# Expert results stored by token through an indirect transfer, and read back as plain rows

## The chip, the cores and the metric

The kernel runs on one core of a Trainium2 chip. The core has five engines that run side by side and meet only through semaphores: the matrix engine (PE), the vector engine (DVE), the scalar engine (ACT), the GpSimd engine (POOL) and the sync engine (SP), whose work here is to issue transfers. Transfers are issued by SP, ACT or POOL and carried out by 16 DMA engines. A transfer whose rows are picked by a list of indices is always issued by POOL in this kernel (`indirect_dma_start`). The metric is the device time of one execution, in microseconds (us); lower is better.

## The reference

Four images of 384 channels and 32 x 32 positions pass through two layers, all in fp32. Layer 0 is attention with relative-position tables and a factored feed-forward block. Layer 1 is a depthwise 7x7 convolution and a mixture of experts over the tokens (one token for each position, 4096 in all). What matters for this change is the mixture:

```python
scores = jnp.einsum('bsd,de->bse', x, gate_w) + gate_b
probs = jax.nn.softmax(scores, axis=-1)
topk_vals, topk_idx = jax.lax.top_k(probs, TOP_K)        # 2 of 4 experts
...
masked = masked / (jnp.sum(masked, axis=-1, keepdims=True) + 1e-09)
h = jax.nn.gelu(jnp.einsum('bsd,edh->ebsh', x, w1) + b1[:, None, None, :], approximate=False)
y = jnp.einsum('ebsh,ehd->ebsd', h, w2) + b2[:, None, None, :]
out = jnp.einsum('bse,ebsd->bsd', masked, y)
```

The kernel computes only the two experts that each token chose. So a token has two result rows of 384 numbers, and its output is the sum of the two, each times its gate.

## The kernel before, in words

**The phases.** `qkv_phase` normalises the input and computes queries, keys and values, eight steps of 512 tokens. In its steps 2 to 5 it also writes zeros over `xs_d`, a DRAM tensor with room for every expert's list of tokens (4 x 4096 rows of 384 numbers, L186 to L190). `attention_phase` is the longest phase. `rest_phase` holds everything after it: projection and feed-forward (`front`), the convolution on DVE (`convolve`, L984) and the experts.

**From tokens to blocks.** For each image, `gates` chooses the experts, and `slot_positions` (L683) gives every token-expert pair a place in that expert's list. `scatter` (L1121) then writes the normalised token rows to these places in `xs_d`, 16 indirect transfers of 128 rows for each image (`write`, L1102). `block_list` (L758) cuts the lists into blocks of 128 rows of one expert. There are 67 blocks in four groups of 13, 16, 16 and 22; group b can start once the rows of image b have landed, for which the loads wait through `after` (L857, used in L1151).

**A block.** `blocks` (L1141) works through a group. `fetch` (L1145) gathers a block's 128 rows into `xg` by an indirect transfer. `turn` (L1155) transposes them on PE and copies them out on ACT as `xT`. Twelve rounds over the hidden units follow: three matmuls (`e_ps`, L1198), a gelu on ACT (`eh`, L1201), a matmul into `y_ps` (L1176). The weights come in halves of 2.5 MB, again by indirect transfers on POOL (`weights`, L1164); where a buffer already holds that expert's half, the indices lie outside and nothing is moved. After the last round, `second` adds the bias on DVE into `yo` (L1179), and SP stores `yo` to rows n to n+127 of `y_d`, so the results lie in the order of the blocks (L1181).

**Back to tokens.** `result_rows` (L736) works out on DVE, from the ranks kept for each image and the `pieces` that `block_list` kept, in which row of `y_d` each token's two results lie. `combine` (L1213) takes 256 tokens at a time: `results` gathers the two rows of each token with four indirect transfers on POOL (L1237) and loads the residual; `weigh` scales and adds (ACT L1249, DVE L1250); `finish` transposes on PE (L1226), adds the residual on DVE (L1227) and stores the output (L1228). Images 0 to 2 are combined in the last group, from its seventh block on (`NOT_LAST`), between the matmuls of the blocks; image 3 is combined after the last block, with all its 16 gathers issued at once.

**What sets the order.** `others` yields small pieces of the next image's work, and `more` (L1357) hands them out between the rounds of a block, by an account of estimated DVE and PE time. Within an engine, the framework's scheduler may move an instruction ahead of one that it expects to wait; across engines only semaphores order the work. Each engine carries out its own queue strictly in order, so an instruction that waits holds up all that is behind it. POOL's queue in `rest_phase` holds the scatters, the gathers of rows, the weight loads and the gathers of results; SP's holds the loads of `front`, the stores of `yo`, the residual loads and the output stores.

Of the kernel before, what the change touches and what calls it, by code (L numbers as in the profile page):

```python
# [47 lines left out]
CAP = B * N  # L48

# [16 lines left out]
def token_stats(nc, pools, ident, x, eps, rows=None, step=4):  # L66
# [5 lines left out]
    for j in range(nj):  # L72
# [6 lines left out]
        if rows is not None:  # L79
            nc.scalar.copy(rows[j], ps[:, :C])  # L80
# [40 lines left out]
def qkv_phase(tc, cst, x, w_qkv, qk_d, v_d, xs_d):  # L121
# [6 lines left out]
    with ExitStack() as es:  # L128
# [7 lines left out]
        zero = wp.tile([P, 1, C], F32, name="zero")  # L136
# [546 lines left out]
def slot_positions(nc, pools, cst, image, count, total):  # L683


    small, psum = pools
# [12 lines left out]
    rank, pos = image["rank"], new(shape, "pos")  # L699
# [15 lines left out]
    for i, pick in enumerate(chosen(nc, new, mask)):  # L715
        for src, dst in ((pos, fpos), (top, image["gate"])):
            nc.vector.tensor_tensor(prod, pick, src, ALU.mult)
            nc.vector.tensor_reduce(dst[:, :, i : i + 1], prod, AX.X, ALU.add)
    nc.vector.tensor_copy(image["pos"], fpos)
# [14 lines left out]


def result_rows(nc, small, image, pieces):  # L736


    shape = list(image["mask"].shape)

    def new(shape, name):
        return small.tile(shape, F32, tag=f"p_{name}", name=f"p_{name}", bufs=1)

    pos, part, step = new(shape, "pos"), new(shape, "prod"), new([P, 1, NEXP], "step")
    nc.vector.tensor_tensor(pos, image["rank"], bcast(pieces[0][1].unsqueeze(1), 1, shape[1]), ALU.add)
    for (_, off0), (lo, off) in zip(pieces, pieces[1:]):
        nc.vector.tensor_tensor(step[:, 0, :], off, off0, ALU.subtract)
        nc.vector.tensor_tensor(part, image["rank"], bcast(lo.unsqueeze(1), 1, shape[1]), ALU.is_ge)
        nc.vector.tensor_tensor(part, part, bcast(step, 1, shape[1]), ALU.mult)
        nc.vector.tensor_tensor(pos, pos, part, ALU.add)  # L750
    row = new([P, shape[1], 2], "fpos")
    for i, pick in enumerate(chosen(nc, new, image["mask"])):
        nc.vector.tensor_tensor(part, pick, pos, ALU.mult)
        nc.vector.tensor_reduce(row[:, :, i : i + 1], part, AX.X, ALU.add)
    nc.vector.tensor_copy(image["pos"], row)


def block_list(nc, small, cst, group, parts, done):  # L758
# [24 lines left out]
    for i, (lo, _, falling) in enumerate(parts):  # L783
        turn = slice(None, None, -1) if falling else slice(None)
        begin, off = group["pieces"][i]
        nc.vector.tensor_scalar(begin, lo, float(BLK), None, ALU.mult)
        nc.vector.tensor_scalar(
            off, first[:, i * NEXP : (i + 1) * NEXP, 0][:, turn], float(group["start"]), float(BLK), ALU.add, ALU.mult
        )
        nc.vector.tensor_tensor(off, off, begin, ALU.subtract)  # L790
# [20 lines left out]
    nc.vector.scalar_tensor_tensor(where, over, OUTSIDE, where, ALU.mult, ALU.add)  # L811
    nc.vector.tensor_scalar(where, where, slot[:, 0:1], cst["wrow"][:, 0:1], ALU.add, ALU.add)
# [22 lines left out]
def rest_phase(tc, cst, x, ao_d, ins, xs_d, y_d, x2_d, out):  # L835
# [9 lines left out]
    with ExitStack() as es:  # L845
# [31 lines left out]
        pc = {"before": const("before", [P, P]), "blocks": const("blocks", [P, MAXB]), "wrow": const("wrow", [P, 2])}  # L877
        pc["one"], pc["slot0"] = one, const("slot0", [P, NEXP])
# [181 lines left out]
        for b, nb in enumerate(COUNTS):  # L1060
# [3 lines left out]
                "rank": new([P, nj, NEXP], f"rank{b}"),  # L1064
# [6 lines left out]
                "pieces": [  # L1071
                    (new([P, NEXP], f"begin{b}{i}"), new([P, NEXP], f"off{b}{i}")) for i in range(1 + (b + 1 == B))
                ],
# [8 lines left out]
        scattered = []  # L1082

        def gates(b):
# [9 lines left out]
            for j, row in enumerate(rows):  # L1094
                nc.scalar.activation(row, row, AF.Identity, bias=shift[:, j, :], scale=rstd[:, j, :])
                im["rows"].append(row)
            yield 0.0, 0.0

        def new_row():
            return hid.tile([P, C], F32, tag="rows", name="rows", bufs=16)  # L1100
# [20 lines left out]
        def scatter(b, pause):  # L1121
            im, g = images[b], groups[b]
            slot_positions(nc, (small, ps_m), pc, im, counts[b], counts[b + 1])
            yield 4.0, 0.5
            for j, rows in enumerate(im["rows"]):
                for s in range(2):
                    write(rows, im["pos"][:, j, s : s + 1])
# [13 lines left out]
        def blocks(g, more):  # L1141
# [3 lines left out]
            def fetch(k):  # L1145
                xg = ld.tile([P, C], F32, tag="xg", name="xg")
# [8 lines left out]
            def turn(k):  # L1155
# [6 lines left out]
                xT[k] = t  # L1162
# [11 lines left out]
            def second(k, ff, hs, w, py):  # L1174
                o = WB + ff % FH * C
                nc.tensor.matmul(py, hs, w[:, o : o + C], start=(ff == 0), stop=(ff == NF - 1))  # L1176
                if ff == NF - 1:
                    yo = hid.tile([P, C], F32, tag="yo", name="yo", bufs=2)
                    nc.vector.tensor_tensor(yo, py, w[:, WB + FH * C :], ALU.add)  # L1179
                    n = (g["start"] + k) * BLK  # L1180
                    nc.sync.dma_start(y_d[n : n + BLK, :], yo)  # L1181
# [5 lines left out]
            for k in range(g["nb"]):  # L1187
                py = ps_y.tile([P, C], F32, tag="y", name="y_ps", bufs=2)
                for ff in range(NF):
# [6 lines left out]
                    for c in range(KC):  # L1196
                        o = c * FH * P + f * P
                        nc.tensor.matmul(ph, w[:, o : o + P], xT[k][:, c, :], start=(c == 0), stop=(c == KC - 1))  # L1198
# [14 lines left out]
        def combine(bs):  # L1213
# [4 lines left out]
            y_rows = y_d if end else y_d[: (groups[-1]["start"] + NOT_LAST) * BLK]  # L1218
            pieces = [p for g in groups for p in g["pieces"]]
# [10 lines left out]
            def results(b, n0):  # L1230

                zs = []
                for j in range(2):
                    ys = [new_row() for _ in range(2)]
                    for i, y in enumerate(ys):
                        index = images[b]["pos"][:, n0 // P + j, i : i + 1]
                        nc.gpsimd.indirect_dma_start(y, None, y_rows, bass.IndirectOffsetOnAxis(ap=index, axis=0))  # L1237
# [8 lines left out]
            def weigh(b, n0, zs):  # L1246
                for j, (z, y) in enumerate(zs):
                    gate = images[b]["gate"][:, n0 // P + j, :]
# [225 lines left out]
```

## Time and profile before

| | |
|---|---|
| median of 3 runs | 3289.18 us (3285.77 to 3293.74) |
| profiled execution | 3284.5 us, span 3282.7 us from first to last instruction |
| PE busy | 2986.8 us, 91% of the span, 25591 matmuls |
| DVE busy | 1991.4 us, 61% |
| ACT busy | 1331.7 us, 41% |
| POOL busy | 1159.6 us, 35% |
| mean granted clock of PE | 0.968 |
| store of `yo` to `y_d` | 67 transfers of 192 KB, issued by SP |
| gathers of results from `y_d` | 64 indirect transfers, issued by POOL |
| zeros to `xs_d` | 8 transfers of 3072 KB, issued by POOL |

The shares are averages over stages with quite different limits. The stages are, by the trace: the qkv phase up to about 237 us, attention up to about 1660 us, the first image's front and convolution up to about 1905 us, the blocks of the experts from there to 3251 us with the other images' fronts and convolutions between them up to about 2600 us, and the last image's combine up to 3282.7 us. Busy time in the views does not count the issue of plain transfers[...].

### The profile page before, as it was taken

The numbers are of one execution on the slowest core, as the hardware profiler recorded it, in microseconds if no ns is written. First come the engines' busy times: TensorE is split into PE (matmuls) and PEld (weight loads), VectorE is DVE, ScalarE is ACT, GpSimd is POOL, SyncE is SP. The second block draws the span as 40 slices with busy tenths as digits, with TensorE's granted clock in tenths as the row PEclk, the third lists the DMA queues.
The fourth block names the chain that finished last, engine by engine and source line by source line (L and its number), as shares of the span: only waits on it lengthen the run. The fifth ranks groups of instructions, "written<-read, shape, count | busy, mean of one in ns | idle before, by whom it ended". The sixth has DMA issues, their size and how long they took to land.

```text
span 3282.7 us, 64040 instructions
## 1 busy us (share of the span) xinstructions
PE 2986.8 (91%) x25591; PEld 2063.8 (63%) x25591; DVE 1991.4 (61%) x3619; ACT 1331.7 (41%) x2687; POOL 1159.6 (35%) x1100
## 2 busy tenths in 40 slices
PE   8998998989898989999879888998999999999996
PEld 4445666666675656666643445575577777777775
DVE  2227777768676877777748659998999730001101
ACT  1115656555555655565511131342443333233322
POOL 2225536263536364544520032123125231114422
PEclk9999999999999999999989998998999999999998
DMA  3786464545455555646240313261156035474852
GB/s 140 268 300 195 102 194 115 179 122 174 117 174 129 169 136 141 171 120 187 74 153 23 113 66 142 80 257 56 44 209 234 27 115 213 152 277 151 303 208 70
DMA packets 222202, 500.60 MB, mean 152 GB/s; under 512 B 92192, under 2 KB 145056, under 8 KB 214224
## 3 DMA queue, kind: packets, MB, share of 16 engines
q1 hardware_dynamic: 156720, 214.75, 21.4%
q0 software_dynamic: 43552, 228.24, 18.8%
q10 hardware_dynamic: 21632, 53.52, 6.4%
q8 instruction: 202, 3.31, 0.4%
q14 instruction: 96, 0.79, 0.1%
HBM read 543.58 MB, written 152.37 MB: 212 GB/s over the span
## 4 chain that ended last, share of the span: by engine, by line
PE 65%; DVE 12%; issue 8%; ACT 7%; DMA 5%; POOL 3%; SPq 1%; another core or an unknown queue 0%; ACTq 0%; POOLq 0%; DVEq 0%
PE e_ps L1198 14%; PE y_ps L1176 13%; DVE xb L993 7%; PE av_ps L215 6%; PE t_ps L406 6%; PE tabq_ps L215 5%; PE sc_ps L215 4%; PE tv_ps L215 3%; ACT arow L387 3%; PE tabk_ps L215 2%; PE qk_ps L163 2%; ACT aT L407 2%; PE a_ps L416 2%; DVE oT L470 2%; DMA qs<-qk_d 1%
## 5 line engine op out<-in xcount | busy, mean ns | idle before, releaser
L349 POOL TENSOR_TENSOR bias<-b,s 128x416 f32<-128x416 f32 (+24 forms) x656 | 660.0, 1043 | 631.8 <-DMA s<-sd 424.5
L1198 PEld LDWEIGHTS e_ps<-xT,w 128*128 128x128 f32 x4824 | 654.6, 192 | 230.5 <-issue 16.7
L1198 PE MATMUL e_ps<-xT,w 128*128 128x128 f32 x4824 | 672.6, 277 | 20.2 <-DVE xb L906 8.0
L1176 PE MATMUL y_ps<-w,eh 128*128 128x384 f32 x1608 | 652.5, 490 | 17.7 <-ACT eh L1201 14.3
L993 DVE SCALAR_TENSOR_TENSOR xb<-img,c_w,xb 128x1024 f32<-128x1024 f32 (+1 forms) x539 | 611.0, 1196 | 0.0
L1201 ACT ACTIVATE eh<-e_ps,w 128x128 f32<-128x128 f32 x804 | 293.3, 367 | 753.8 <-PE e_ps L1198 692.3
L1166 POOL DMA_INDIRECT w<-in_w,row x134 | 164.0, 1224 | 786.4 <-PE y_ps L1176 270.7
L377 DVE CUSTOM_DVE_ANT_0 arow<-sc_ps,bias 128x1024 f32<-128x1024 f32 x256 | 312.8, 1222 | 191.4 <-POOL bias L349 101.9
L398 DVE TENSOR_REDUCE extra<-arow 128x32 f32<-128x32 f32 (+24 forms) x768 | 378.7, 551 | 30.2 <-ACT arow L387 30.2
L406 PEld LDWEIGHTS t_ps<-ident,arow 128*128 128x128 f32 x2048 | 226.4, 144 | 265.0 <-ACT arow L387 185.3
L407 ACT COPY aT<-t_ps 128x512 f32<-128x512 f32 x512 | 275.5, 589 | 267.4 <-PE t_ps L406 241.9
L387 ACT ACTIVATE arow<-arow,nm 128x1024 f32<-128x1024 f32 x256 | 297.0, 1160 | 177.6 <-DVE nm L377 166.5
L406 PE MATMUL t_ps<-ident,arow 128*128 128x128 f32 x2048 | 289.1, 286 | 74.4 <-ACT arow L387 73.3
L215 PE MATMUL sc_ps<-kk,qs 48*32 48x512 f32 x4096 | 294.0, 625 | 50.8 <-DMA qs<-qk_d 26.8
L1179 DVE TENSOR_TENSOR yo<-y_ps,w 128x384 f32<-128x384 f32 x67 | 37.2, 556 | 446.9 <-PE y_ps L1176 439.7
L1176 PEld LDWEIGHTS y_ps<-w,eh 128*128 128x128 f32 x1608 | 248.0, 193 | 31.1 <-ACT eh L1201 16.9
L215 PEld LDWEIGHTS av_ps<-aT,vb 128*64 128x64 f32 x4096 | 222.3, 137 | 52.3 <-ACT aT L407 37.8
L303 DVE STREAM_TRANSPOSE b<-tabk_ps 128x480 f32<-128x480 f32 x256 | 219.1, 1000 | 44.5 <-PE tabk_ps L215 24.8
L215 PE MATMUL av_ps<-aT,vb 128*64 128x128 f32 x4096 | 237.7, 274 | 0.0
L215 PE MATMUL tabk_ps<-tab,kq 48*128 48x480 f32 x512 | 225.7, 588 | 3.3 <-DVE b L303 3.3
L215 PE MATMUL tabq_ps<-tab,kq 48*128 48x480 f32 x512 | 224.5, 585 | 0.7 <-ACT va L177 0.7
L308 ACT COPY st<-tabq_ps 128x480 f32<-128x480 f32 x256 | 141.8, 561 | 75.3 <-PE tabk_ps L215 36.5
(212 smaller groups left out, 3190.4 us busy)
## 6 DMA issues: line engine op xcount, KB each, us to landing
sd<-st SPq DMA_DIRECT2D x128, 480.0 KB
s<-sd SPq DMA_DIRECT2D x512, 120.0 KB
xs_d<-zero POOLq DMA_DIRECT2D x8, 3072.0 KB
tvw<-in_tv ACTq DMA_DIRECT2D x120, 192.0 KB
y_d<-yo SPq DMA_DIRECT2D x67, 192.0 KB
qk_d<-qk_sb POOLq DMA_DIRECT2D x48, 256.0 KB
qs<-qk_d SPq DMA_DIRECT2D x256, 48.0 KB
kq<-qk_d ACTq DMA_DIRECT2D x56, 192.0 KB
```

Source lines behind the costliest of these rows:

```text
L215: ins = nc.tensor.matmul(*args, **kw)
L303: turn = nc.vector.transpose(b2.rearrange("p e y x -> p x (e y)")[:, i + j], ps[:, j, : SPAN * IMG])
L349: nc.gpsimd.tensor_tensor(bias[:, y0:y1, :], bass.AP(b2.tensor, b2.offset + (e * IMG + y0) * IMG, [list(b2.ap[0]), [(step * IMG + 1) * IMG ...
L377: nc.vector.tensor_tensor_reduce(s["flat"], ps.rearrange("p h n -> p (h n)"), s["bias"].rearrange("p y x -> p (y x)"), -SCALE, BIG, ALU.ad ...
L387: nc.scalar.activation(s["flat"], s["flat"], AF.Exp, bias=s["nm"], scale=-1.0, accum_out=dn[:, y % YT : y % YT + 1])
L398: pin(nc.vector.tensor_reduce(ex[:, i, :], a[:, p0:p1, :].rearrange("p y x -> p x y"), AX.X, ALU.add))
L406: pin(nc.tensor.transpose(pt[:, j, :], s["flat"][:, k0 : k0 + P], ident))
L407: pin(nc.scalar.copy(aT[:, 4 * g : 4 * g + 4, s["y"] % YB, :], pt))
L993: nc.vector.scalar_tensor_tensor(acc[:, k, y0:y1], img[:, k, dy + y0 : dy + y1, dx : dx + IMG], w7[:, k, dy, dx : dx + 1], acc[:, k, y0:y1 ...
L1176: nc.tensor.matmul(py, hs, w[:, o : o + C], start=(ff == 0), stop=(ff == NF - 1))
L1198: nc.tensor.matmul(ph, w[:, o : o + P], xT[k][:, c, :], start=(c == 0), stop=(c == KC - 1))
L1201: nc.scalar.activation(hs, ph, AF.Gelu, bias=w[:, o : o + 1])
```

## The change

The result of a block no longer goes to the block's rows, but to its token's rows: `z_d` has two rows for each token, row 2t for the first of its two experts and 2t+1 for the second.

- **Rows carry their address.** The rows of `xs_d` become 386 numbers long (`CX`). `scatter` appends two numbers to each row: twice the token's index less `OUTSIDE`, and the list start of the token's first expert. The token numbers come as a constant. `slot_positions` computes the second with two more DVE operations, `scatter` the first with one, and ACT copies both into the row (one small copy for each 128 rows). The zeros written over `xs_d` have the new row length too.
- **A block works out where its rows go.** In `turn`, two small DVE operations on 128 x 1 numbers compare the block's expert with the row's first expert and add up the row of `z_d`; empty slots end up outside and are skipped.
- **The store.** `second` stores `yo` with an indirect transfer on POOL, in place of the plain one on SP.
- **The loads.** `results` loads every second row of 256 rows of `z_d` with plain transfers: on SP, and in the last image's combine half of them on ACT. They wait, through `after`, for the stores of the blocks that can hold their tokens (`written`).
- **Removed.** `result_rows`, the `pieces` and the `rank` that it needed, and `y_d`. The combine of images 0 to 2 starts once the stores of all the blocks that can hold their tokens are issued, which is at the same block as before.

```diff
-        zero = wp.tile([P, 1, C], F32, name="zero")
+        zero = wp.tile([P, 1, CX], F32, name="zero")
...
+        if i == 0:
+            nc.vector.tensor_tensor(prod, pick, bcast(cst["slot0"].unsqueeze(1), 1, nj), ALU.mult)
+            nc.vector.tensor_reduce(image["ids"][:, :, 1:2], prod, AX.X, ALU.add)
...
-def result_rows(nc, small, image, pieces):
...
+    nc.vector.tensor_scalar(group["over"], over, OUTSIDE, OUTSIDE, ALU.mult, ALU.add)
+    nc.vector.tensor_scalar(group["first"], expert, float(CAP), None, ALU.mult)
...
+            nc.vector.tensor_scalar_add(im["ids"][:, :, 0], pc["token"], 2.0 * b * N)
             yield 4.0, 0.5
             for j, rows in enumerate(im["rows"]):
+                nc.scalar.copy(rows[:, C:], im["ids"][:, j, :])
...
-                xT[k] = t
+                at = small.tile([P, 1], F32, tag="at", name="at")
+                nc.vector.tensor_tensor(at, g["first"][:, k, :], xg[:, C + 1 :], ALU.is_gt)
+                to = small.tile([P, 1], U32, tag="to", name="to", bufs=3)
+                nc.vector.scalar_tensor_tensor(to, at, g["over"][:, k, :], xg[:, C : C + 1], ALU.add, ALU.add)
+                xT[k] = t, to
...
-                    n = (g["start"] + k) * BLK
-                    nc.sync.dma_start(y_d[n : n + BLK, :], yo)
+                    stored.append(nc.gpsimd.indirect_dma_start(
+                        to_z.pop(), bass.IndirectOffsetOnAxis(ap=xT.pop(k)[1], axis=0), yo, None,
+                        bounds_check=2 * NT - 1, oob_is_err=False,
+                    ))
...
-                        index = images[b]["pos"][:, n0 // P + j, i : i + 1]
-                        nc.gpsimd.indirect_dma_start(y, None, y_rows, bass.IndirectOffsetOnAxis(ap=index, axis=0))
+                        r0 = 2 * (b * N + n0 + j * P) + i
+                        queue = nc.scalar if end and i else nc.sync
+                        load = queue.dma_start(y[:, :C], from_z[r0 : r0 + 2 * P - 1 : 2, :])
+                        for other in written:
+                            after(load, other)
...
-            if not end:
-                for b in (*bs, B - 1):
-                    result_rows(nc, small, images[b], pieces)
-                    yield 3.0, 0.0
...
-            if g is groups[-1] and k == NOT_LAST and "combined" not in g:
+            if len(stored) == groups[-1]["start"] + NOT_LAST and "combined" not in groups[-1]:
                 g["combined"] = combine(range(B - 1))
...
-    xs_d = dram.tile([NEXP * CAP, C], F32, name="xs_d")
-    y_d = dram.tile([ALL * BLK, C], F32, name="y_d")
+    xs_d = dram.tile([NEXP * CAP, CX], F32, name="xs_d")
+    z_d = dram.tile([2 * NT, C], F32, name="z_d")
```

## The prediction

> **What bounds the kernel now.** I read the page's shares first (PE busy 91% of 3282.7 us), then the busy time of each engine by stage, and then the timeline wherever a stage touches the change. By stage:
>
> ```profile
> 150.00:160.00 10.00, 7.56 (x19) 3.23 (x17) 0.00 (x0) 1.40 (x3) 1.61 (x3) 1.00 1.01 359
> ...
> 2160.00:2260.00 100.00, 93.45 (x541) 69.22 (x539) 98.86 (x201) 36.59 (x85) 31.06 (x26) 0.98 0.52 196
> 2660.00:2760.00 100.00, 100.00 (x616) 79.81 (x615) 3.63 (x8) 30.20 (x81) 22.05 (x22) 1.00 0.52 194
> 2960.00:3060.00 100.00, 97.27 (x607) 77.89 (x607) 15.12 (x27) 33.89 (x88) 43.78 (x44) 1.00 0.59 213
> 3252.00:3283.00 31.00, 7.57 (x24) 4.25 (x24) 8.76 (x16) 4.92 (x8) 15.46 (x16) 0.55 0.53 156
> ```
>
> The columns are the stretch, its length, then busy us of PE, PE's weight loads, DVE, ACT and POOL, PE's clock, the DMA engines' share and GB/s. From 2660 to 2960 PE is never idle: what the change adds to POOL or DVE there costs nothing, and what it takes from SP brings nothing. Four places are not covered by PE: the qkv phase after 120 us (DMA engines full, PE idle), the conv stretch to about 2260 (DVE full), the combine of images 0 to 2 (small PE gaps), and the end, where PE works 7.6 of 31 us.
>
> The end, from the timeline:
>
> ```profile
> 3250.38 0.56 DVE L1179 TENSOR_TENSOR yo<-y_ps,w 128x384 f32<-128x384 f32 x1 [13.89 <-PE y_ps L1176]
> 3253.64 0.97 POOL L1237 DMA_INDIRECT rows<-y_d,pos  x1 [31.68 <-issue]
> ...
> 3256.81 0.61 ACT L1249 ACTIVATE rows<-rows,gate 128x384 f32<-128x384 f32 x1 [7.94 <-DMA rows<-y_d,pos]
> ...
> 3272.72 0.96 POOL L1237 DMA_INDIRECT rows<-y_d,pos  x1 [0.30 <-issue]
> ```
>
> The store takes 2.70 us from the end of `yo` to the first gather; then POOL issues 16 gathers, one in 1.27 us, until 3273.7. ACT and DVE work a row as it lands. POOL's issue is the limit.
>
> The start of group 1:
>
> ```profile
> 2236.86 1.02 POOL L1103 DMA_INDIRECT xs_d<-rows,pos  x1 [21.77 <-DVE b_first L782]
> ...
> 2245.20 0.54 DVE L1179 TENSOR_TENSOR yo<-y_ps,w 128x384 f32<-128x384 f32 x1
> ...
> 2261.81 1.02 POOL L1147 DMA_INDIRECT xg<-xs_d,slot  x1 [1.01 <-DMA xs_d<-rows,pos]
> ...
> 2265.04 0.88 PE L1160 MATMUL xT_ps<-ident,xg 128*128 128x128 f32 x3 [7.52 <-DMA xg<-xs_d,slot]
> ```
>
> A chain from DVE over POOL to PE: PE stands 7.52 us. What is added ahead of it on DVE or POOL comes out of PE's time.
>
> [...] an indirect issue takes about 1.0 us with DVE idle and up to 2.1 us beside the convolution, while the convolution's operation keeps its 1.28 us.
>
> **The change part by part.** All against the profiled execution (span 3282.7, time 3284.5); the median of the runs, 3289.2, lies 4.7 above, and I carry the difference over to it.
>
> *The end, -8.5 us.* `yo` ends at 3250.94. The scatter waits on nothing else in POOL's queue: 0.1 for the semaphore, 1.0 to issue, and 2.36 to land (row above: the last scatter of image 1 was issued by 2259.45, the gather waiting for it started at 2261.81). Loads start at 3254.4, 0.8 later than the gathers. A plain issue takes 0.32 us (the store's row); eight on SP and eight on ACT are out after 3 to 5 us instead of 20. The first pair lands at about 3257, as before, but ACT issues its eight first and turns to scaling at about 3258.5. After that two limits: DVE has 8 x 0.62 + 4 x 1.02 = 9.0 us and about 2.5 us of waits for PE's transposes, so 3258.5 + 0.6 + 11.5 = 3270.6; and the DMA engines, 16.4 us of full work in this stretch (shares times lengths), from 3255.2 to 3271.6. The last output then takes 3.5 us to the end of the span (3279.2 to 3282.7 now): about 3274.2. Bounds: -4 if[...] the outputs queue behind them on SP, -11 if both limits overlap well.
>
> *Combine of images 0 to 2, -4 us.* 48 gathers of 1.27 us leave POOL, where they stood ahead of weights and `xg`; the loads wait on SP, where only residuals and outputs are behind them. The last 16 blocks take 277.1 us between `yo` rows (2973.27 to 3250.38); undisturbed ones take 16.11 each, 257.8. Of the 19.3 over, the 72 transposes (0.137 each) are 9.9 and stay; 9.4 are gaps. Not all of these come from late rows, as some waits name no partner. I take not quite half. Bounds: 0 and -9.
>
> *`result_rows`, -1 us.* Four times about 35 DVE operations at 0.1 to 0.2 us, run near 2640 to 2665, where PE has short waits; DVE has 30% free, so nearly all was covered. Bounds 0 and -3.
>
> *DVE in the conv stretch, +3 us.* Two 128x1 operations for each block; small ones take 0.15 to 0.17 us, and about 0.1 when packed. 0.2 for each of 13 blocks is 2.6, plus 0.3 for the operations on the ids. DVE is 97 to 99% busy there and starts the chain at 2236. After 2400 PE covers it (16.1 us each block). Bounds +1 and +5. A row that lands late would stall DVE at the first of the two, but PE's transposes at the same place in the program waited on `xg` once only (7.5 us, that above).
>
> *POOL, +1.3 us.* In most blocks the store stands before the weight half that waits for the same `yo` (256.6 us of such waits), so the weights come 1.3 to 2 us later; they are needed some 20 us later. At the end of group 0 it stands among the 16 scatters of image 1, behind which group 1 waits: one issue more, 1.3 us. If it stands there before `yo` is ready at 2245.74, the rest of the scatters wait as well, 4 to 8 us. Bounds 1 and 8; I take the low end, since the scheduler moves ready work forward.
>
> *Start of group 0, +0.3 us*: three DVE operations and an ACT copy ahead of the first scatter; the other copies run beside POOL's 1.28 us for each scatter.
>
> *Zeros, +2 us.* The chain in the qkv phase, cut to one round:
>
> ```profile
> 163.61 1.17 POOL xs_d L190
> 164.78 11.81 issue
> 176.59 0.02 POOLq L168
> ```
>
> POOL stands[...]; stores of `qk_d`, and so DVE and PE, stand behind. 25.2 MB of zeros at about 360 GB/s are 70 us of full DMA engines, and PE idles 8.4 us between 150 and 240. Each per cent on a zero row costs 0.7 us.[...] Bounds +1.4 and +12; I take 3%[...].
>
> SP loses 67 stores, and nothing that PE waits for was behind them. Sum: -8.5 - 4 - 1 + 3 + 1.3 + 0.3 + 2 = -6.9. Span about 3275.8; median 3289.2 - 6.9 = 3282.
>
> **Rivals.** *Rows of 1544 B (slower).*[...] For it: the DMA engines stand at share 1.0 and PE is idle there. Against: the bytes grow by 0.5%. At 28% more for each row it costs 20 us: 3289 - 9 + 20 = 3300. It decides from about 22% on, where 15.5 us make up for the -8.9 of the rest and 6.6 more. *A wait for a wait:* the last store of group 0 holds the scatters (8 us), or the end gains no more than 4 and the combine nothing: about 3290. For it: POOL's strict order; against: moved-up work elsewhere in the trace. *All gaps go:* -11 at the end and -9 in the combine: 3289.2 - 20 - 1 + 6.6 = 3275; for it, the loads leave the weights' queue.
>
> **How the numbers follow.** Forecast 0.48 (3276 to 3288), all gaps 0.20, a wait for a wait 0.12, rows of 1544 B 0.20. About 0.2%, 6.6 us, is what a measurement tells from no change. The forecast's case lies 0.28 beyond it and 0.20 within; with 0.20 and 0.08 from the rivals that is 0.48 faster and 0.28 the same. Slower 0.24: 0.20, and 0.04 of the wait. The range runs from 3269 (all gaps, with some luck) to 3301.
>
> **What would show it.** First scaling on ACT 6 to 9 us after the last `yo`, and the span's end about 23 us after it instead of 32; loads issued within 5 us. PE gaps after 2973 below 7 us. PE's wait at the start of group 1 some 4 us longer. PE idle 150 to 240 about 10 us; 20 or more proves the rows. Wrong would make me: a zero transfer's pace changed by over 10%, ACT held by its own issues at the end, or stores waiting on POOL before the scatters.

## The result, and the profile after

| | before | after |
|---|---|---|
| median | 3287.47 us (3279.6 to 3293.74, 4 runs) | 3319.77 us (3318.74 to 3320.12, 4 runs) |
| ratio, 95% interval | | 1.0099 (1.0076 to 1.0122) |
| profiled execution, span | 3284.5 us, 3282.7 us | 3320.12 us, 3318.4 us |
| PE busy | 2986.8 us, 91% | 2997.1 us, 90% |

The change costs 32 us, where I had forecast a gain of 7. The median of the kernel before differs by up to 1.1% between chips (3260.07 to 3295.88 us), so each run below has its ratio to the kernel before on its own chip. In the changed kernel the lines have moved: `yo` is L1166, the store L1167, the weights L1153, the fetch L1129, the scatter L1083, the gelu L1190, the loads of results L1226, their scaling L1241 (ACT) and L1242 (DVE), the transposes out L1214.

Busy time by stage of the changed kernel; columns as in the prediction.

```profile
150.00:160.00 10.00, 8.97 (x24) 4.08 (x22) 0.00 (x0) 1.75 (x3) 4.16 (x6) 1.00 0.83 294
2160.00:2260.00 100.00, 98.56 (x604) 76.28 (x604) 98.45 (x200) 41.77 (x105) 25.83 (x18) 1.00 0.51 193
2660.00:2760.00 100.00, 91.13 (x534) 72.26 (x535) 13.11 (x86) 32.41 (x90) 38.29 (x38) 0.97 0.42 157
3000.00:3100.00 100.00, 82.62 (x475) 64.14 (x475) 21.52 (x44) 33.87 (x84) 19.00 (x19) 0.91 0.67 230
3296.00:3318.00 22.00, 6.81 (x24) 4.37 (x24) 8.36 (x16) 4.37 (x8) 0.13 (x1) 0.54 0.63 218
```

The combine of images 0 to 2 (3000 to 3100), in which PE should have lost its small gaps, is where PE now stands 17.4 of 100 us. POOL, which the change was to relieve there, works 19.0 us instead of 43.8, and the stage is longer all the same.

Where the 35.7 us between the two spans lie, from the starts of the attention's first table matmul, of its last pair of value-table matmuls, and of the `yo` rows (numbered 1 to 67) in both timelines:

| stretch | before | after | difference | forecast |
|---|---|---|---|---|
| to the first table matmul (zeros) | 237.20 | 239.96 | +2.8 | +2 |
| attention, to its last value-table pair | 1414.09 | 1417.16 | +3.1 | 0 |
| from there to `yo` 1 | 324.97 | 334.55 | +9.6 | +0.3 |
| `yo` 1 to 13 (group 0) | 268.94 | 271.61 | +2.7 | +3 |
| `yo` 13 to 14 (start of group 1) | 71.52 | 79.86 | +8.3 | +1.3 |
| `yo` 14 to 30 | 294.24 | 295.66 | +1.4 | 0 |
| `yo` 30 to 32 (start of group 2) | 56.38 | 60.50 | +4.1 | -1 |
| `yo` 32 to 51 | 305.93 | 305.30 | -0.6 | 0 |
| `yo` 51 to 67 (combine of images 0 to 2) | 277.11 | 289.69 | +12.6 | -4 |
| `yo` 67 to the end | 32.32 | 24.11 | -8.2 | -8.5 |

Of the +2.8 in the first row, 0.8 lies ahead of the first projection matmul (25.2 and 26.0 us), before any zero is written; the start of that matmul lies between 24.4 and 26.0 us in all the profiles. What is left for the zeros is 2.0. The attention, whose code is the same in all runs, takes 1411 to 1426 us in the profiles, so its +3.1 says nothing.

**The end**, from the timeline of the changed kernel (ACTq and SPq are transfers being issued):

```profile
3294.29 0.56 DVE L1166 TENSOR_TENSOR yo<-y_ps,w 128x384 f32<-128x384 f32 x1 [13.89 <-PE y_ps L1163]
3295.13 1.01 POOL L1167 DMA_INDIRECT z_d<-yo,to  x1 [12.95 <-DVE yo L1166]
...
3297.69 7.11 SPq L1226 DMA_DIRECT2D rows<-z_d  x8
3297.77 1.78 ACTq L1226 DMA_DIRECT2D rows<-z_d  x4
3300.36 0.61 ACT L1241 ACTIVATE rows<-rows,gate 128x384 f32<-128x384 f32 x1 [7.59 <-DMA rows<-z_d]
3300.81 4.24 ACTq L1226 DMA_DIRECT2D rows<-z_d  x4
3305.09 3.14 ACT L1241 ACTIVATE rows<-rows,gate 128x384 f32<-128x384 f32 x6 [4.11 <-DMA rows<-z_d]
```

The loads are out after 7.4 us instead of 20, and the span ends 24.1 us after the last `yo`. ACT scales one row and then issues its other four loads in 4.24 us; the second scaling starts at 3305.

**The zeros**, one round of the chain in the qkv phase of the changed kernel:

```profile
166.41 1.17 POOL xs_d L191
167.59 11.65 issue
179.24 0.02 POOLq L169
```

The wait is 11.65 us where it was 11.81, and from 150 to 240 us the DMA engines move 306 GB/s in both kernels: a longer row has not made the zero transfers slow.

**The first image's front.** First the kernel before, then the changed kernel, from the timelines of DVE and POOL:

```profile
1688.19 10.85 POOL L1019 TENSOR_TENSOR w<-half,c_w 128x3136 f32<-128x3136 f32 x2 [9.31 <-DVE b_first L780]
1688.85 4.80 DVE L775 SCALAR_TENSOR_TENSOR b_slot<-done,c_slot 128x4 f32<-128x4 f32 x1
1693.58 1.02 DVE L77 BATCH_NORM_STATS2 s_st<-row_ps 128x6 f32<-128x384 f32 x2
```

```profile
1693.71 10.85 POOL L998 TENSOR_TENSOR w<-half,c_w 128x3136 f32<-128x3136 f32 x2 [9.44 <-DVE b_first L763]
1694.37 10.29 DVE L1104 TENSOR_SCALAR ids<-c_token 128x8 f32<-128x8 f32 x4
1704.57 1.02 DVE L78 BATCH_NORM_STATS2 s_st<-row_ps 128x6 f32<-128x384 f32 x2
```

The four additions of the token numbers (L1104) read only a constant. The scheduler has moved all four, for all images, from the images' slot chains to this place, where POOL multiplies the diagonal weights. They are done when POOL's second product is, and the normalisation of image 0 waits behind them. In the kernel before one small operation stood there, until POOL's first product ended (1693.6). The trace shows no wait ahead of the additions: two of the four are long in themselves, 4.82 and 5.41 us, where the shortest takes 0.16. The text at the top, by which the engines meet only through semaphores, does not cover this.

**The start of group 1**, from the timelines of the changed kernel:

```profile
2258.15 0.99 POOL L1083 DMA_INDIRECT xs_d<-rows,pos  x1 [6.63 <-ACT eh L1190]
...
2263.28 0.55 DVE L1166 TENSOR_TENSOR yo<-y_ps,w 128x384 f32<-128x384 f32 x1
...
2274.78 1.00 POOL L1167 DMA_INDIRECT z_d<-yo,to  x1 [0.30 <-DVE pause L978]
...
2286.15 1.02 POOL L1129 DMA_INDIRECT xg<-xs_d,slot  x1 [1.44 <-DMA xs_d<-rows,pos]
...
2289.45 0.87 PE L1142 MATMUL xT_ps<-ident,xg 128*128 128x128 f32 x3 [12.63 <-DMA xg<-xs_d,slot]
```

The first scatter comes 5.1 us ahead of the group's last `yo` and not 8.3. From it to the first fetch it is 28.0 us instead of 24.95. PE stands 12.63 us, 5.1 more than before.

**The combine of images 0 to 2**, from the timelines and the waits (us in total, times, longest) of the changed kernel:

```profile
3049.53 0.81 PE L1214 MATMUL out_ps<-ident,rows 128*128 128x128 f32 x6
3051.70 0.35 ACT L1190 ACTIVATE eh<-e_ps,w 128x128 f32<-128x128 f32 x1
3053.92 9.90 SPq L1226 DMA_DIRECT2D rows<-z_d  x2
3062.21 0.61 ACT L1241 ACTIVATE rows<-rows,gate 128x384 f32<-128x384 f32 x1 [10.17 <-DMA rows<-z_d]
3062.73 0.35 ACT L1190 ACTIVATE eh<-e_ps,w 128x128 f32<-128x128 f32 x1
...
3083.49 0.61 ACT L1241 ACTIVATE rows<-rows,gate 128x384 f32<-128x384 f32 x1 [5.21 <-DMA rows<-z_d]
...
3094.78 0.61 ACT L1241 ACTIVATE rows<-rows,gate 128x384 f32<-128x384 f32 x1 [7.99 <-DMA rows<-z_d]
```

```profile
ACT rows L1241 <- DMA rows<-z_d: 29.3, 10, 10.2
PE y_ps L1163 <- ACT eh L1190: 16.2, 3, 7.8
```

ACT stands 10.17 us at one scaling whose row was issued only at 3053.9, and the next gelu runs right after it, at 3062.73. Four blocks in a row take 21.4, 26.4, 22.9 and 21.6 us; an undisturbed one takes 16.1. In the kernel before, ACT never stood at a scaling in this stage.

### The profile page after: what moved, and what is told of

Read it like the earlier page. It is cut to its first block, busy times and chain, and to the rows that moved or that the text cites. A ratio compares the mean times of both kernels' runs of the same rounds, so it can differ in the third digit from the quotient of the medians.

```text
span 3318.4 us, 64231 instructions
## 1 busy us (share of the span) xinstructions
PE 2997.1 (90%) x25591; PEld 2071.7 (62%) x25591; DVE 1999.8 (60%) x3646; ACT 1333.7 (40%) x2719; POOL 1177.6 (35%) x1103
## 4 chain that ended last, share of the span: by engine, by line
PE 65%; DVE 12%; issue 7%; ACT 6%; DMA 6%; POOL 2%; SPq 1%; another core or an unknown queue 0%; ACTq 0%; POOLq 0%; DVEq 0%
PE e_ps L1187 14%; PE y_ps L1163 13%; DVE xb L972 7%; PE av_ps L216 6%; PE t_ps L407 5%; PE tabq_ps L216 5%; PE sc_ps L216 4%; PE tv_ps L216 3%; PE tabk_ps L216 2%; ACT arow L388 2%; PE qk_ps L164 2%; ACT aT L408 2%; PE a_ps L417 2%; DVE oT L471 2%; DMA rows<-z_d 1%
## 5 line engine op out<-in xcount | busy, mean ns | idle before, releaser
L1163 PE MATMUL y_ps<-w,eh 128*128 128x384 f32 x1608 | 654.7, 493 | 30.7 <-ACT eh L1190 29.3
L1190 ACT ACTIVATE eh<-e_ps,w 128x128 f32<-128x128 f32 x804 | 293.1, 367 | 740.5 <-PE e_ps L1187 691.8
L1166 DVE TENSOR_TENSOR yo<-y_ps,w 128x384 f32<-128x384 f32 x67 | 37.1, 554 | 440.7 <-PE y_ps L1163 417.1
L1167 POOL DMA_INDIRECT z_d<-yo,to x67 | 85.3, 1273 | 532.7 <-DVE yo L1166 306.7
L1153 POOL DMA_INDIRECT w<-in_w,row x134 | 162.7, 1214 | 304.9 <-PE y_ps L1163 238.6
```

The costliest lines, as they stand in the source:

```text
L1190: nc.scalar.activation(hs, ph, AF.Gelu, bias=w[:, o : o + 1])
```

## The experiments

### The order of the scalings

```diff
-                    nc.scalar.activation(z, z, AF.Copy, scale=gate[:, 0:1])
+                    tc.keep_in_program_order(nc.scalar.activation(z, z, AF.Copy, scale=gate[:, 0:1]))
```

The call pins an instruction behind all that the program has written on its engine so far. Behind the attention, POOL's order stays the same to the instruction and PE's all but; the DVE additions that use the scaled rows move with the scalings.

> The changed kernel, with one edit: ScalarE's scaling of the loaded rows in the combine of images 0 to 2 is held in the order in which the program writes it; the scheduler had moved it ahead of the gelus around it. Theory A (ScalarE stands at scalings placed before their rows can have landed, the gelus queue behind them and TensorE stops): the four block intervals of 21 to 26 us in that stage go back to 16 to 18 us, TensorE's wait for gelus there falls from 29 us to under 8, ScalarE's waits for loads from 41 us to under 10, and the time falls by 15 to 27 us, to 3293 to 3305. Theory B (the loads are late because of the traffic, and whoever needs them stands): the same waits appear in the blocks after, and the time stays within 6 us of 3320.

Measured: 3298.34 us, ratio 1.0014 (1.0005 to 1.0023). `yo` 51 to 67 takes 267.1 us instead of 289.7, with no block over 19.3 us. (The 29 and 41 us of waits in the expectation are those of the whole program; in this stage they are the 16.2 and 29.3 above.) The operations on the loaded rows, in the changed kernel and then in this run: count, shortest, median and longest ns, first and last start.

```profile
L1241 ACT ACTIVATE rows<-rows,gate x24: 602/614/617, 3023.7 to 3094.8; 128x384 f32<-128x384 f32 x24
```

```profile
L1241 ACT ACTIVATE rows<-rows,gate x24: 602/606/619, 3023.4 to 3169.0; 128x384 f32<-128x384 f32 x24
```

The scheduler had put all 24 scalings into 71 us, where the program spreads them over 146 and the transposes that use the rows and free their buffers stay spread. So ACT came to a scaling before its load could have a buffer, or have landed. All PE waits left between `yo` 51 and 67 in this run:

```profile
PE e_ps L1187 <- ACT xT L1143: 0.6, 1, 0.6
```

Theory A holds: the wait was in the order, not in the rows' landing. No run pins the scalings in the kernel before.

### The order of the additions

```diff
-            nc.vector.tensor_scalar_add(im["ids"][:, :, 0], pc["token"], 2.0 * b * N)
+            tc.keep_in_program_order(nc.vector.tensor_scalar_add(im["ids"][:, :, 0], pc["token"], 2.0 * b * N))
```

> The changed kernel, with one edit: VectorE's adds of the token numbers are held in program order, so that they run with their image's slot chain and not ahead of the first normalisation at about 1694 us. Theory A (the hoisted adds stand for 10.3 us and the first normalisation behind them): the first normalisation after the attention starts 5 to 10 us sooner, and the time falls by 5 to 10 us, to 3310 to 3315. Theory B (another of the small hoisted operations takes over the wait, since what they wait for is the GpSimd operation that runs at the same time or a constant): the start moves by under 2 us and the time stays at 3318 to 3321.

Measured: 3308.22 us, ratio 1.0049 (1.0032 to 1.0067). The timelines of POOL and DVE in this run:

```profile
1694.97 10.85 POOL L998 TENSOR_TENSOR w<-half,c_w 128x3136 f32<-128x3136 f32 x2 [9.40 <-DVE b_first L763]
1696.27 1.03 DVE L78 BATCH_NORM_STATS2 s_st<-row_ps 128x6 f32<-128x384 f32 x2 [0.56 <-PE row_ps L76]
1697.30 3.13 DVE L758 SCALAR_TENSOR_TENSOR b_slot<-done,c_slot 128x4 f32<-128x4 f32 x1
```

The normalisation starts 1.3 us after POOL's products instead of 10.9, and from the attention's last pair to `yo` 1 it is 319.6 us instead of 334.6. Of these 15 us, 8.8 lie ahead of the first block's fetch; the other 6.1 lie between the fetch and the block's first transposes, where no addition runs and ACT's waits differ from profile to profile. A, with a small part of B: the next hoisted operation stands 3.13 us, until POOL's first product ends.

### Longer rows alone

The kernel before, with these edits and slices to 384 where the row is used:

```diff
-            return hid.tile([P, C], F32, tag="rows", name="rows", bufs=16)
+            return hid.tile([P, CX], F32, tag="rows", name="rows", bufs=16)
...
+            for row in rows:
+                nc.gpsimd.memset(row[:, C:], 0.0)
...
-    xs_d = dram.tile([NEXP * CAP, C], F32, name="xs_d")
+    xs_d = dram.tile([NEXP * CAP, CX], F32, name="xs_d")
```

> The kernel before, with the expert rows made 386 words long instead of 384 (zero rows, scattered rows and fetched rows alike; two unused words at the end, set to zero by GpSimd) and nothing else. Theory A (a longer row costs only its share of the zeros, 2 to 3 us before the attention): first attention matmul 2 to 4 us later, group starts as before, time 3288 to 3293. Theory B (a row of 1544 bytes is slow in the scatters and fetches too): each of the four group starts 2 to 4 us later, time 3295 to 3303. Theory C (no cost): 3284 to 3288.

Measured: 3285.62 us, ratio 0.999 (0.9975 to 1.0005). The first table matmul comes at 239.50, 2.3 us later; 0.7 of that lies ahead of the first projection matmul, so the zeros cost 1.6. From the attention's last pair to `yo` 1 it is 323.0, the start of group 1 71.9, the combine 276.7, all within 2 us of the kernel before. So theory A in the stages; the time lies in theory C's range, and 1.6 us are too little for the times to tell. A row of 1544 bytes costs some 2 us in the zeros and nothing measurable in scatters and fetches.

### The store off POOL

```diff
-                    stored.append(nc.gpsimd.indirect_dma_start(
-                        to_z.pop(), bass.IndirectOffsetOnAxis(ap=xT.pop(k)[1], axis=0), yo, None,
-                        bounds_check=2 * NT - 1, oob_is_err=False,
-                    ))
+                    n = (g["start"] + k) * BLK
+                    stored.append(nc.sync.dma_start(to_z.pop()[n : n + BLK, :], yo))
...
```

> The changed kernel, with the blocks' results stored as plain consecutive rows through SyncE's queue, as in the kernel before, instead of by token through GpSimd's; target rows are still worked out on VectorE, but not used, so the combine reads rows in the wrong order and the output is not the reference's. It takes the store off GpSimd's queue alone. Theory A (group 1 starts 8.3 us later because VectorE's added operations make the slots later and the store sits among the scatters at 1.3 us): the start of group 1 is still 5 to 7 us later than before. Theory B (waiting for a store holds the scatters and fetches behind it): the start of group 1 is within 2 us of the kernel before. The combine's stall stays in both, so the time is 3310 to 3320.

Measured: 3306.10 us, ratio 1.0054 (1.0032 to 1.0077), below the 3310 to 3320 expected. The start of group 1 takes 76.4 us, 4.9 more than before, just under theory A's 5; the combine 286.5. It seemed to price the stores there at 3.5 us, which the later experiment on the store did not confirm.

### Both orders; targets on ACT; one queue at the end; one order more

Both edits above together:

> The changed kernel with both order edits (the rows' scaling on ScalarE and the token numbers' adds on VectorE held in program order). If the two losses are separate they add: 21 us and 11 us off 3320, so 3286 to 3290 where the kernel before has 3287 to 3292, a ratio of 0.996 to 1.000. If the one hides the other (the time given back ahead of group 0 is lost again in the combine), the ratio stays above 1.001.

With them, on ACT:

```diff
-                nc.vector.tensor_tensor(at, g["first"][:, k, :], xg[:, C + 1 :], ALU.is_gt)
+                nc.scalar.activation(at, xg[:, C + 1 :], AF.Sign, bias=g["first"][:, k, :], scale=-1.0)
+                nc.scalar.activation(at, at, AF.Identity, bias=g["over"][:, k, :])
...
-                nc.vector.scalar_tensor_tensor(to, at, g["over"][:, k, :], xg[:, C : C + 1], ALU.add, ALU.add)
+                nc.scalar.activation(to, xg[:, C : C + 1], AF.Identity, bias=at)
```

> As the run with both order edits, and the target row of each block is worked out on ScalarE (sign, add, add: three small operations behind the copy of the transposed rows) and no longer on VectorE (a compare and an add). Theory A (VectorE, which the convolution fills in groups 0 to 2, carries the two operations of each block onto the path and makes the scatter slots of the next image late): group 0 is 2 to 3 us shorter and the start of group 1 4 to 5 us shorter, 6 to 9 us in all. Theory B (what makes group 1 start late is the store among the scatters and the longer slot chain): under 3 us. Theory C (ScalarE in its order holds the gelus up): slower by up to 5 us.

With both orders, all loads of the end on SP:

```diff
-                        queue = nc.scalar if end and i else nc.sync
+                        queue = nc.sync
```

> As the run with both order edits, and the 16 loads of the last image's rows are all issued by SyncE, where the changed kernel gives half of them to ScalarE. If the two queues matter, the stretch from the last block's result to the end grows by 16 issues at about 0.9 us less 8 of them, that is by 3 to 7 us from 24 to 25.5. If the rows' landing and the scaling set it whatever the queue, it stays within 1 us.

With both orders, and `b_slot` pinned as well, the operation that stood beside POOL's product in the kernel before and in the run with the additions pinned (`pin` is `keep_in_program_order`):

```diff
-        nc.vector.scalar_tensor_tensor(
+        pin(nc.vector.scalar_tensor_tensor(
             slot[:, own], lo[:, turn], float(BLK), cst["slot0"][:, turn], ALU.mult, ALU.add
-        )
+        ))
```

> As the run with both order edits, and one more small VectorE operation held in program order: the first of the block list, which reads only constants and stood 4.8 us in the kernel before and 3.1 us in the run with the adds in order, while GpSimd's two long products ran. Theory A (each small hoisted operation[...] stands until a GpSimd product ends): the first normalisation of image 0 is done 2 to 4 us sooner and the time falls by as much. Theory B (the normalisation's own copies of that kind wait for GpSimd in its place): under 1 us.

Measured, on one chip, where the kernel before has 3261.03 us (15 runs):

| | median | ratio, interval | `yo` 1 to 13 | 13 to 14 | 67 to end |
|---|---|---|---|---|---|
| both orders | 3272.12 | 1.0036 (1.0025 to 1.0048) | 271.7 | 79.8 | 24.6 |
| and targets on ACT | 3284.48 | 1.0070 (1.0057 to 1.0082) | 276.9 | 77.4 | 25.9 |
| and one queue | 3272.29 | 1.0040 (1.0023 to 1.0056) | 272.7 | 79.0 | 22.9 |
| and one order more | 3275.25 | 1.0042 (1.0027 to 1.0056) | 271.7 | 79.9 | 25.1 |

The times answer the first expectation badly: the ratio is above 1.001. But all four combines take 267 us, and the stretch to `yo` 1 takes 319.0 to 324.7, so neither loss had come back in full; the kernel before is some 30 us shorter here than elsewhere, taken up below. Targets on ACT: slower by 12.4 us, the sign of theory C and more than its 5; of the 16.6 us between the two profiles, 5.3 lie behind the attention and 10.9 in it, where the code is the same. The start of group 1 gets 2.3 us shorter and group 0 5.2 longer. As ACT has to do the work instead, this does not say what the two operations cost on DVE. One queue: my expectation had the wrong sign. The timelines at the end of that run:

```profile
3250.95 7.89 SPq L1226 DMA_DIRECT2D rows<-z_d  x16
...
3253.34 0.61 ACT L1241 ACTIVATE rows<-rows,gate 128x384 f32<-128x384 f32 x1 [7.30 <-DMA rows<-z_d]
3255.39 0.61 ACT L1241 ACTIVATE rows<-rows,gate 128x384 f32<-128x384 f32 x1 [1.44 <-DMA rows<-z_d]
```

SP issues all 16 loads in 7.9 us, where the changed kernel needs 7.4 with two queues, and ACT scales the second row 2.05 us after the first instead of 4.7. The end gets about 1.7 us shorter, too little for the times to tell. One order more: theory B, no gain. From the first `s_st` to the first `u` it is 17.4 us, and 17.0 in the run with one queue, whose code is the same there; operations of the normalisation take the wait over. (In the run with both orders itself it is 23.5.)

### The three kernels on one chip

> The kernel before, unchanged, for a profile on the same chip as the two runs that go with it. The attention's length wanders by up to 8 us between profiles in which its code is the same, so stages are compared from the attention's end on: 1631 us in the first profile. If stages are steady from chip to chip, this one has 1629 to 1633.

> The changed kernel, unchanged, on the same chip. From the attention's end on it took 1661 us in its first profile, 30 more than the kernel before; if the causes are in the order of the queues and not in the chip, it is 1659 to 1663 again, and the ratio of the times 1.008 to 1.011.

> The changed kernel with both order edits, on the same chip as the other two of this call. From the attention's end on it took 1622 us, 9 less than the kernel before. If that holds on one chip, the ratio is 0.997 to 1.000 (2 to 3 us of it lost ahead of the attention to the longer zero rows); if the 1.0036 measured on another chip holds, the kernel before must be shorter there in a stage that its first profile did not show, and its profile here shows which.

Measured: before 3295.88 us (21 runs), after 3323.28 us, ratio 1.0087 (1.0066 to 1.0107), both orders 3287.30 us, ratio 0.9977 (0.9967 to 0.9988). Stages from the attention's last pair on:

| stretch | before | after | both orders |
|---|---|---|---|
| to `yo` 1 | 324.7 | 335.7 | 323.1 |
| `yo` 1 to 13 | 268.9 | 271.6 | 270.4 |
| 13 to 14 | 71.5 | 79.7 | 79.2 |
| 14 to 30 | 294.3 | 295.7 | 294.6 |
| 30 to 32 | 56.4 | 59.4 | 61.9 |
| 32 to 51 | 305.9 | 305.2 | 305.2 |
| 51 to 67 | 277.1 | 291.1 | 267.1 |
| 67 to the end | 32.1 | 24.7 | 25.0 |
| together | 1630.8 | 1663.2 | 1626.4 |

The losses repeat, and two pins turn +32.4 into -4.4: on this chip the version with both orders beats both kernels. What was forecast as -4 in the combine is -10.0 here with both orders pinned. PE's waits in that stage of the kernel before are these and one of 1.2 us; with both orders pinned none is left there.

```profile
PE y_ps L1176 <- ACT eh L1201: 5.7, 3, 2.7
PE out_ps L1226 <- DVE rows L1250: 1.9, 2, 1.3
```

### The store among the scatters, once more

With both orders, the stores of the last two blocks of a group are kept and issued after the next group's first fetch and weights:

```diff
...
+                    if g is not groups[-1] and k >= g["nb"] - 2:
+                        kept.append(store)
+                    else:
+                        store()
...
             turn(0)
+            while kept:
+                kept.pop(0)()
```

> As the run with both order edits, and the stores of the last two blocks of each group but the last are written into the program after the next group's first fetch and weights, so that none stands among the 16 scatters. Theory A (a store among the scatters delays the first fetch of group 1 by its issue and what the scatters behind it lose, 3.5 us between the run with plain stores and the changed kernel): the scatters take 21.6 to 22.3 us instead of 24.2 to 25.2, and the start of group 1 falls from 79 us to 75 to 77. Theory B (the scatters' own landing and the longer slot chain set it): 78 to 80, as before.

Measured: 3278.45 us, ratio 1.0044 (1.0027 to 1.0061), again on the chip of the four runs above, where the kernel before now has 3263.81. POOL's timeline at the start of group 1:

```profile
2246.59 0.99 POOL L1084 DMA_INDIRECT xs_d<-rows,pos  x1 [6.52 <-ACT rows L1108]
...
2268.92 1.75 POOL L1084 DMA_INDIRECT xs_d<-rows,pos  x1 [0.30 <-issue]
...
2273.83 1.01 POOL L1130 DMA_INDIRECT xg<-xs_d,slot  x1 [1.81 <-DMA xs_d<-rows,pos]
```

The 16 scatters take 24.1 us without a store among them, 25.4 with one in the run with both orders, 22.6 in the kernel before; the start of group 1 is 79.1 us. Theory B: the store is worth its issue, about 1.3 us, and no more.

### Where the kernel before is short

> The kernel before, unchanged. From the attention's end on it took 1631 us in two profiles. If the chip on which it takes 3261 us is the one drawn, theory A (ScalarE's unnamed waits around the scatters, 14 us in all in the first profiles, are not there, as in the three other profiles of that chip) gives 1613 to 1619 from the attention's end and the rest of the 30 us in the attention; theory B (the attention alone is shorter) gives 1629 to 1633.

> The changed kernel, unchanged, beside it. Whatever the chip, the two losses of the orders stay: 10.3 us of VectorE at the token adds and four blocks of 21 to 28 us in the combine; the ratio is 1.008 to 1.012.

Measured, on a second such chip: before 3260.07 us (7 runs), after 3301.93 us, ratio 1.0133 (1.0114 to 1.0152), above what I expected. From the attention's last pair on the kernel before takes 1605.4 us, even less than theory A had it, and the changed kernel 1647.9. The kernel before is shorter than in the last table by 11.5 us to `yo` 1, by 7.7 from `yo` 30 to 32 and by 8.4 from 51 to 67; the changed kernel by 7.6, 7.3 and 0.4. ACT's timeline during the scatters of image 0, first in the kernel before on the earlier chip, then on this one:

```profile
1904.77 1.31 ACT L944 ACTIVATE hs<-f_ps 128x512 f32<-128x512 f32 x2 [4.43 <-remote]
1909.65 0.60 ACT L944 ACTIVATE hs<-f_ps 128x512 f32<-128x512 f32 x1 [3.57 <-remote]
```

```profile
1893.43 1.57 ACT L944 ACTIVATE hs<-f_ps 128x512 f32<-128x512 f32 x3 [0.78 <-PE f_ps L934]
1895.48 1.58 ACT L944 ACTIVATE hs<-f_ps 128x512 f32<-128x512 f32 x3 [0.48 <-PE f_ps L934]
```

"remote" is a releaser that the profile can't name. Over the whole program such waits of ACT add up to 15.4 us in the first of the two and to nothing in the second. With a combine of 268.7 us in the kernel before, the 267.1 us of the version with both orders on the other short chip are 1.6 less and not 10. PE's waits in the combine of the kernel before add up to 2.5 us here, none of them for a gelu.

The two short profiles also show what lies in the start of group 0, as no unnamed wait covers it there. It takes 14.9 us longer in the changed kernel: 5.9 up to the fetch of the first block's rows, 8.9 from there to the first transposes of these rows (9.8 and 18.7 us), nothing after. In between, from the timelines of DVE and PE, first the kernel before, then the changed kernel:

```profile
1904.45 0.69 DVE L923 TENSOR_TENSOR u<-u_ps,scale 128x512 f32<-128x512 f32 x1 [1.88 <-PE u_ps L921]
1905.20 1.99 PE L934 MATMUL f_ps<-u,c_c_fc 32*128 32x512 f32 x12 [0.84 <-DVE u L923]
```

```profile
1915.61 0.16 DVE L1146 TENSOR_TENSOR at<-first,xg 128x1 f32<-128x1 f32 x1 [20.01 <-DMA xg<-xs_d,slot]
...
1915.94 2.06 DVE L931 SCALAR_TENSOR_TENSOR xb<-ffn_ps,c_c_proj,xb 128x512 f32<-128x512 f32 x3
1917.91 0.68 DVE L902 TENSOR_TENSOR u<-u_ps,scale 128x512 f32<-128x512 f32 x1
1918.65 3.78 PE L913 MATMUL f_ps<-u,c_c_fc 32*128 32x512 f32 x12 [7.08 <-DVE u L902]
```

DVE stands 20.0 us at `at`, the first of the two operations that work out where a block's rows go, until the fetched rows have landed. Behind it in DVE's queue stand operations of the next image's front, and PE, which needs them, stands 7.08 us where it stood 0.84. On the first chip the changed kernel has this stand with 21.2 us, and the run with the late stores has it with 20.0. With the targets on ACT it is ACT that stands at `at`: 26.65 us at the start of group 1. No run puts the two operations behind the front's.

The runs with both orders on the other short chip keep PE's wait (7.0 us in the run with the late stores), and their stretch to `yo` 1 is 5.2 to 11.5 us longer than that of the kernel before here. With their later group 1, this can make the version with both orders slower on such chips.

## Why the prediction was wrong

**"Combine of images 0 to 2, -4 us" failed.** Measured +12.6. The step priced what leaves POOL and where the loads stand, and took their readers to stay where they were. The readers moved: the scheduler packed the 24 scalings into half their stretch, ACT waited in order, and the gelus and PE behind it. With both orders pinned it is -10.0 on the same chip, below the lower bound of -9, and -1.6 between the two short chips. So the gain is there once the order is kept, but it is not shown to come from the step's own mechanism, the gathers that leave POOL: PE's named waits in this stage of the kernel before were 8.8 us where it gains 10.0 and 2.5 where it gains 1.6, and most of the difference is 5.7 us for gelus, not for rows. My list of what would make me wrong had ACT "held by its own issues at the end", not by rows in this stage.

**"Start of group 0, +0.3 us" failed.** Measured +9.6, of which 3.5 lie ahead of the first fetch and 6.0 behind it. I counted three DVE operations and placed them ahead of the first scatter. One of them has only a constant as input, and the scheduler was free to run it for all four images 190 us and more ahead of its place, beside POOL's products. What holds a DVE operation there is not shown, as no run takes the products away. The traces agree in time: the additions end at 1704.66 us and POOL's second product at 1704.56; `b_slot` ended with the first product, at 1693.65 and 1693.6 in the kernel before, and at 1700.4 both with the additions pinned. I had priced such an operation at 0.1 to 0.2 us and never asked what runs beside it.

The other part is a term put at nothing. "A row that lands late would stall DVE", I wrote, and set it aside because PE had waited on such rows "once only". DVE stood 61.9 us at `at`, in 17 places: 38.6 of them after `yo` 32, where DVE has time (from 2660 it is busy 13.1 of 100 us), and 21.2 at the start of group 0. There the row could not land before 16 scatters had, while DVE had the next image's work behind it; on the short chip PE lost 6.2 us more for that work than in the kernel before. How much it is on the other chips, where ACT's unnamed waits fall into the same stretch, is not told apart.

**"POOL, +1.3 us" was right as a price and too small as a step.** A store among the scatters costs about 1.3 us (they take 25.4 us with one and 24.1 without). The start of group 1 is later by 8.3 us all the same: the first scatter by 3.2 in relation to `yo`, the 16 scatters by 2.6 with the store among them, the fetch behind them by 0.4, and the first block by 2.0. Putting the last two stores elsewhere brought nothing; with the two operations on ACT the start was 2.3 us shorter. What makes the rest is open. The forecast "PE's wait at the start of group 1 some 4 us longer" held (5.1), but it is not the whole of the start. The 4.1 us between `yo` 30 and 32 I had not foreseen either; there the waits change with the chip.

**Right:** *zeros*, 2.0 for +2 once the 0.8 ahead of them is taken off; PE idles 9.8 us from 150 to 240, as said, and the rival of slow rows falls. The 3% on a row were my estimate, with no trace behind it; 2.0 of the 70 us that I had counted for the zeros are 2.9%. *`result_rows`*, -1, is not to be told apart.

**Right in the sum, with some luck:** *the end*, -8.2 for -8.5. The loads took 7.4 us to issue and not 3 to 5. The first scaling came 6.1 us after the last `yo`, but ACT then turned back to issuing, and scaled on only 10.2 us after the end of `yo` instead of 7.6; DVE was done 9.6 us after that instead of 12.1. The two errors cancel. *DVE in the conv stretch*, +2.7 for +3 in group 0: DVE is busy 1.3 us more and waits 1.4 us more, where I had put it all down to work.

**The rivals.** "Rows of 1544 B" had the sign, at 3300, and the wrong cause: it put 20 us on the zeros, which lost 2.0. "A wait for a wait", near 3290, had the kind of cause, but its place was POOL's queue at the last store of group 0; the waits that came were ACT's and DVE's, for loads. No case reached 3320.

## What to carry to other kernels

Where a scheduler orders the queues, an edit also changes what it believes to be ready: list the instructions that the edit lets run early (here four that read only a constant, and the readers of loads that had become plain transfers; why the scheduler moved the latter is not shown), and ask what each would stand in front of on its engine. Ask the same of a small operation that is new and reads what a transfer brings: on a busy engine it costs what waits behind it (DVE stood 20.0 us at `at`, and PE 7.08 us for what was queued behind). When a change that takes work away makes a kernel slower, look for an in-order engine that stands at a load while others wait for what is queued behind it (ACT stood 10.17 us at one scaling, and PE 7.85 us for the gelu behind); pinning one instruction is the test, and here it was the cure for two of the three waits. Price a wait on more than one chip before a gain of 0.2% is called one: the combine's was 10.0 us on one chip and 1.6 between two others.

## What the hardware showed that I had not expected

- A DVE addition over 128 x 8 numbers took up to 5.41 us while POOL worked on a product of 5.4 us, and 0.16 us without one. What holds it is not shown.
- The kernel before takes 3287 to 3296 us on some chips and 3260 to 3264 on two others, with PE's clock at 0.967 and 0.972 in the two profiles compared. Of ACT's waits with a releaser that the profile can't name, 15.4 us are in the one profile and none in the other. What ACT waits for is open.
- Two issuing queues were hardly faster than one: 16 loads left SP alone in 7.9 us, and two queues took 7.4, with one scaling among ACT's issues.
- Rows of 1544 bytes instead of 1536 cost 1.6 to 2.0 us in 25 MB of zeros, counted from the first projection matmul, and nothing measurable in scatters and fetches.
